# A planned attention and spiking block: counts summed onto x, the first rotation on VectorE, and a plan with varied durations

## The chip, the cores and the metric

The kernel runs on one core of one Trainium2 chip. The metric is device time in microseconds: the median of the runs of one program. The profile is one execution more, taken by the hardware profiler.

## The reference

The input x has 16 batches of 1,024 tokens of 256 features. A causal attention with 16 heads of 16 features and rotary positions, and a spiking feed-forward part, both read the normalised x; both results are added to x.

```python
xn = _layernorm(x, axis=-1)
x = x + _L0_attn_ref(xn, Wq, bq, Wk, bk, Wv, bv, Wo, bo, token_positions) \
      + _L0_ffn_ref(xn, W_fc, W_proj)
# attention: Q, K rotated; softmax(Q K^T / 4, causal) V, then Wo and bo
# feed-forward: 5 steps on the same y
h = jnp.square(jax.nn.relu(jnp.einsum('bsd,fd->bsf', x, W_fc)))
y = jnp.einsum('bsf,df->bsd', h, W_proj)
def step(mem, _):
    reset = spike_fn(mem - THRESHOLD)
    mem_new = BETA * mem + y - reset * THRESHOLD
    return (mem_new, spike_fn(mem_new - THRESHOLD))
_, spks = jax.lax.scan(step, mem0, None, length=NUM_STEPS)
return jnp.sum(spks, axis=0) / NUM_STEPS
```

Since y is the same in all five steps, the number of spikes is a step function of y: the kernel compares y with five constants (`LEAST`) and counts how many it exceeds.

## The kernel before

**Arithmetic.** The f32 factors of a product are split into f16 pairs, a high part and a remainder, and `three` (L587 to L592) makes three f16 matmuls of each product. Weights carry a scale, 256 for the projections and 320 (`WO_S`) for the output projection.

**Stages of a batch.** `norms` reads x two chunks of 128 tokens at a time, normalises, splits into `xhl` and turns it to `xT` by a transposing DMA (L627). `rotated` makes q and k: per half of the tokens and for q and k, two products into PSUM, ACT adds the bias into `qk` (L670), then sine product into `ms` and cosine product into `qk` (L678), difference and sum (L686), the high part on ACT (L733), the remainder (L689), and two stores to a scratch in DRAM, `scr` (L693, L697). `load_slots` brings 4 heads at a time back as `qS` and `kS` (L783). `largest` computes all scores once to find each row's maximum (matmuls L803, VectorE L819 and L837), `weighted` computes them again (L920), takes the exponential on ACT (L981), masks on POOL (L938) and multiplies by the values in f32 (L947); the values carry a column of ones for the softmax sum. Four times per batch a result goes through DRAM to be divided by its sum and split into `ahl`. `forward` is the feed-forward part: product with W_fc, relu and squares on ACT and POOL, product with W_proj into `py`, and `spikes`. `projected` is the output projection: per two chunks one PSUM bank `po`, then `onto` adds it to x, and a DMA stores the result.

**The counts before.** `spikes` writes a f16 tile `count`, by one comparison (L1147) and four that add (L1152), all VectorE over 128x512. Later, in `projected`, TensorE multiplies `count` by a scaled identity `fifth` into `po` ahead of the 12 matmuls of the projection (L1041). There x is loaded (L1066), POOL adds bo (L1068), and VectorE's `onto` adds `po`, over 320, to x (L1059).

**The first rotation before.** `combined` (L381) gives an element-by-element operation to POOL. For batch 0 the rotation is cut in two halves of 512 elements, and each half may be taken by VectorE or by POOL, whichever the plan finds free.

**What sets the order.** Nothing is issued where it is written. `Plan.op` (L155) records an operation with its engine, a planned duration (`cost`), a due time (`when`), and what it reads and writes. `Plan.order` (L193) then plays the whole kernel through with these durations: whenever an engine is free in the plan, it takes the ready operation that is due first, if buffers and PSUM banks allow, and TensorE prefers to stay in its array mode (whole array, split in rows for the scores, split in columns for L947). The order of this play becomes the order of each engine's queue; on the chip every queue runs strictly in that order. Due times come from a period of 140e3 per batch (`BATCH`); the play begins near `S0` = -70e3, and `SMALL` = 60e3 is when wo, bv and bo are loaded. SP issues all DMAs but one, in one queue.

Of the kernel before, what the change touches and what calls it, by code (L numbers as in the profile page):

```python
# [3 lines left out]

# [17 lines left out]
P = 128  # L22
H = 16
# [15 lines left out]
WO_S = 320.0  # L39
# [46 lines left out]
BUFS = dict(w=5, xn=2, x=3, relu=2, ms=2, hT=3, avT=2, ahl=6)  # L86
# [20 lines left out]
SMALL = 60e3  # L107
L1, L2 = 30e3, 25e3
QD = 6.5e3

# [30 lines left out]
class Op:  # L141
    __slots__ = ("mode", "engine", "cost", "when", "what", "held", "waits", "then", "start", "early", "ready", "size", "alt", "name", "patience")


class Plan:
# [9 lines left out]
    def op(self, engine, cost, when, what, reads=(), writes=(), also=(), window=None, size=0.0,  # L155
           alt=(), mode=FULL, patience=PATIENCE):
        o = Op()
        o.mode = mode
        o.size, o.alt, o.patience = size, alt, patience
# [33 lines left out]
    def order(self):  # L193
# [19 lines left out]
        mode = None  # L213

# [50 lines left out]
        while events:  # L265
            now = events[0][0]
            while events and events[0][0] <= now:
                _, _, kind, o = heappop(events)
                if kind == 0:
                    heappush(queues[o.engine], (o.when, o))  # L270
                    if o.alt:
                        heappush(events, (now + o.patience, n, 3, o))
                        n += 1
# [28 lines left out]
            for engine in queues:  # L302
# [7 lines left out]
                if o is not None:  # L310
                    busy[engine] = True
                    o.start = now
                    order.append(o)
                    cost = o.cost
                    if engine == "pe":
                        cost += SWITCH * (o.mode != mode)
                        mode = o.mode
                    heappush(events, (now + cost, n, 1, o))
                    n += 1
# [39 lines left out]
def tile_block(ctx: ExitStack, tc, x, wqkv, bqk, bv, wo, bo, wfc, wproj, cos, sin, out):  # L359
# [21 lines left out]
    def combined(n, when, what, reads, writes, rate=2.27, scalar=None, vector=False):  # L381


        alt, patience = [], PATIENCE
        if scalar is not None:
            alt = [("act", act(n) + 35, scalar)]
        if vector:
            alt, patience = [("dve", dve(n, 2.1), lambda: what(nc.vector))], 0.0
        op("pool", pool_(n, rate), when, lambda: what(nc.gpsimd), reads, writes, alt=alt,
           patience=patience)  # L390
# [46 lines left out]

    fifth = const.tile([P, P], F16, name="fifth")
    nc.vector.tensor_scalar(fifth, ident16, WO_S / NUM_STEPS, None, ALU.mult)

# [106 lines left out]
    def bias_product():  # L547
# [7 lines left out]
    op("dve", dve(D), SMALL + 1e3, lambda: nc.vector.tensor_tensor(bo_sb, pbo.t[:, :D], bo_sb, ALU.add),  # L555
       [pbo, "small"], ["bo"])
# [4 lines left out]
    for i in range(2):  # L561
        t = const.tile([P, NC, H * VW + VT - VW], F32, name=f"v_sb{i}")
        ones = t[:, :, : H * VW].rearrange("p c (h w) -> p c h w", w=VW)[:, :, :, DK]
        nc.gpsimd.memset(ones, 1.0)
        nc.gpsimd.memset(t[:, :, H * VW :], 1.0)
# [9 lines left out]
    class Batch:  # L575
        def __init__(self, b):
# [7 lines left out]
            self.count = [None] * (NC // 2)  # L584
# [10 lines left out]
    def norms(st, times):  # L595
# [36 lines left out]
        for n in range(NC // 2):  # L632
            i = n // (NC // 4)
            t = times[n]
            if n % (NC // 4) == 0:
                for c in range(HALF):
# [14 lines left out]
                   [xn, (hl, 0)], [(hl, 1)], 2.05, vector=b == 0)  # L651
# [3 lines left out]
    def rotated(st, times):  # L655
# [19 lines left out]

        def times_(engine, table, half, to, r, es):
            cols = slice(half * QB, (half + 1) * QB)
            engine.tensor_tensor(  # L678
                to.t[:, es], r.t[:, es],
                table[:, :, cols].broadcast_to([P, es.stop - es.start, QB]), ALU.mult,  # L680
            )

        def added(engine, r, ms, es):
            for e in range(es.start, es.stop):
                a, b = (r.t[:, e, :], ms.t[:, 1 - e, :])[:: 1 if e == 0 else -1]
                engine.tensor_tensor(r.t[:, e, :], a, b, (ALU.subtract, ALU.add)[e])  # L686

        def less(engine, t, r, hl, es):
            engine.tensor_tensor(hl.t[:, 1 - t, es], r.t[:, es], hl.t[:, t, es], ALU.subtract)  # L689
# [12 lines left out]
        for half in range(2):  # L702
            for t in range(2):
# [13 lines left out]
                parts = [slice(0, 1), slice(1, 2)] if b == 0 else [slice(0, 2)]  # L717
                n = 1024 // len(parts)

                def each(after, what, reads, to, mine, rate=2.27):  # L720
                    for es in parts:
                        own = [(to, e) for e in range(2)[es]]
                        combined(n, at + QD + after, lambda e, es=es: what(e, es),
                                 reads if mine is None else [*reads, *((r, e) for e in range(2)[es])],
                                 own, rate, vector=b == 0)

                each(3e3, lambda e, es, half=half, r=r, ms=ms: times_(e, sin_sb, half, ms, r, es),
                     ["sin"], ms, r)
                each(5e3, lambda e, es, half=half, r=r: times_(e, cos_sb, half, r, r, es),
                     ["cos"], r, None)  # L730
                each(8e3, lambda e, es, r=r, ms=ms: added(e, r, ms, es), [(ms, 0), (ms, 1)], r, None)
                op("act", act(1024), at + QD + 10e3,
                   lambda t=t, r=r, hl=hl: nc.scalar.copy(hl.t[:, t], r.t), both, [(hl, t, 0), (hl, t, 1)])  # L733
                for es in parts:
                    es_ = range(2)[es]
                    combined(n, at + QD + 12e3,
                             lambda e, t=t, r=r, hl=hl, es=es: less(e, t, r, hl, es),
                             [*((r, e) for e in es_), *((hl, t, e) for e in es_)],
                             [(hl, 1 - t, e) for e in es_], 2.0, vector=b == 0)
                stored_keys = [(hl, x, e) for x in range(2) for e in range(2)]  # L740
                op("sp", dma(2), at + QD + 13e3, lambda t=t, half=half, hl=hl: stored(t, half, hl),
                   stored_keys, [("scr", b % 2, t, half)], size=move(P * 6 * QB * 2))
# [570 lines left out]
```

## Time and profile before

| | |
|---|---|
| median of 3 runs | 2438.48 us (2437.65 to 2441.66) |
| profiled execution | 2438.26 us, span 2436.6 us |
| mean granted TensorE clock | 0.993 |
| HBM | 122.82 MB read, 101.71 MB written |

The costliest groups (line, engine, operation, written tile, tiles read, shapes, count; then busy time and mean ns of one; then the idle time of the engine just before, with what ended it):

```profile
L981 ACT ACTIVATE w<-banks 128x512 f32<-128x512 f32 (+1 forms) x2560 | 1246.6, 572 | 294.6 <-PE banks L920 280.5
L819 DVE TENSOR_REDUCE nm_sb<-banks 128x1 f32<-128x512 f32 x1024 | 642.6, 683 | 138.8 <-PE banks L803 137.6
L947 PE MATMUL banks<-w,v_sb 128*32 128x512 f32 (+3 forms) x6144 | 622.9, 494 | 3.6 <-DVE nm_sb L819 1.4
```

The granted clock of TensorE over 40 slices of the span, in tenths, and under it the mean busy share of the DMA engines:

```profile
PEclk8999999999999999999999999999999999999999
DMA  5442524433334344344342434233433242432221
```

PE is TensorE's matmuls, PEld its loads of weights, DVE is VectorE, ACT ScalarE, POOL GpSimd and SP the engine that issues DMAs. Matmuls overlap: the duration of one is longer than the time that it holds the array, so the distance from start to start tells its cost. What an idle engine waited for is inferred from semaphores.

### The profile page before, as it was taken

The numbers are of one execution on the slowest core, as the hardware profiler recorded it, in microseconds if no ns is written. First come the engines' busy times: TensorE is split into PE (matmuls) and PEld (weight loads), VectorE is DVE, ScalarE is ACT, GpSimd is POOL, SyncE is SP. The second block draws the span as 40 slices with busy tenths as digits, with TensorE's granted clock in tenths as the row PEclk, the third lists the DMA queues.
The fourth block names the chain that finished last, engine by engine and source line by source line (L and its number), as shares of the span: only waits on it lengthen the run. The fifth ranks groups of instructions, "written<-read, shape, count | busy, mean of one in ns | idle before, by whom it ended". The sixth has DMA issues, their size and how long they took to land.

```text
span 2436.6 us, 59006 instructions
## 1 busy us (share of the span) xinstructions
PE 2356.5 (97%) x21060; PEld 1182.3 (49%) x21060; DVE 1987.8 (82%) x6065; ACT 1843.3 (76%) x3599; POOL 1806.9 (74%) x1922
## 2 busy tenths in 40 slices
PE   5999999999999999999999999999999999999997
PEld 3544444445445445454544445455454444544553
DVE  6888888887987879788788878877878887787882
ACT  5588778787778778777787777787877878777775
POOL 7877757778678877779778587776877858687553
PEclk8999999999999999999999999999999999999999
DMA  5442524433334344344342434233433242432221
GB/s 170 110 102 80 137 80 120 106 89 108 91 119 111 89 100 109 93 110 123 89 115 84 106 113 105 89 96 84 130 98 115 89 103 88 106 113 82 68 68 54
DMA packets 253935, 246.21 MB, mean 101 GB/s; under 512 B 108104, under 2 KB 207816, under 8 KB 253640
## 3 DMA queue, kind: packets, MB, share of 16 engines
q1 hardware_dynamic: 253504, 242.44, 36.2%
q8 instruction: 165, 2.70, 0.5%
q14 instruction: 130, 1.06, 0.2%
q10 hardware_dynamic: 136, 0.00, 0.0%
HBM read 122.82 MB, written 101.71 MB: 92 GB/s over the span
## 4 chain that ended last, share of the span: by engine, by line
PE 58%; DVE 7%; ACT 3%; issue 2%; DMA 1%; POOL 1%; SPq 0%; POOLq 0%; DVEq 0%; ACTq 0%
PE banks L590 27%; PE banks L947 14%; PE banks L920 8%; PE banks L803 8%; DVE junk L837 3%; ACT w L981 2%; DVE nm_sb L819 1%; DVE count L1152 1%; DVE nm_sb L837 1%; PE banks L1041 1%; PE banks L864 0%; ACT hT L1128 0%; POOL hT L1134 0%; DMA av_dram<-avT 0%; DMA inv<-inv 0%
## 5 line engine op out<-in xcount | busy, mean ns | idle before, releaser
L981 ACT ACTIVATE w<-banks 128x512 f32<-128x512 f32 (+1 forms) x2560 | 1246.6, 572 | 294.6 <-PE banks L920 280.5
L819 DVE TENSOR_REDUCE nm_sb<-banks 128x1 f32<-128x512 f32 x1024 | 642.6, 683 | 138.8 <-PE banks L803 137.6
L947 PE MATMUL banks<-w,v_sb 128*32 128x512 f32 (+3 forms) x6144 | 622.9, 494 | 3.6 <-DVE nm_sb L819 1.4
L938 POOL TENSOR_SCALAR_AFFINE_SELECT w<-w 128x256 f32<-128x256 f32 x1024 | 399.3, 408 | 286.9 <-ACT w L981 271.7
L837 DVE CUSTOM_DVE_ANT_0 junk<-banks,mask,nm_sb 128x256 bf16<-128x256 f32 (+3 forms) x1024 | 498.1, 547 | 99.0 <-PE banks L803 61.9
L837 DVE CUSTOM_DVE_ANT_0 junk<-banks,mask 128x256 bf16<-128x256 f32 (+3 forms) x1024 | 444.4, 486 | 64.0 <-PE banks L803 57.2
L920 PE MATMUL banks<-qS,kS 50*128 50x512 f16 (+3 forms) x3072 | 431.7, 328 | 9.6 <-DVE nm_sb L819 3.5
L803 PE MATMUL banks<-kS,qS 48*128 48x512 f16 (+3 forms) x3072 | 415.8, 326 | 9.5 <-DVE nm_sb L837 4.3
L590 PE MATMUL banks<-wproj_hi,hT 128*128 128x256 f16 x2048 | 383.4, 276 | 8.0 <-ACT relu L1123 6.5
L590 PE MATMUL banks<-xT,wfc_hi 128*128 128x256 f16 x2048 | 350.3, 273 | 6.6 <-ACT w L981 2.5
L590 PEld LDWEIGHTS <-hT 128*128 128x128 f16 x3072 | 282.8, 98 | 110.2 <-issue 74.5
L1130 POOL TENSOR_TENSOR relu<-relu 128x1024 f32<-128x1024 f32 x118 | 223.5, 1894 | 125.6 <-ACT hT L1128 125.1
L920 PEld LDWEIGHTS <-kS 50*128 50x128 f16 x3072 | 132.7, 94 | 314.3 <-issue 288.6
L590 PE MATMUL banks<-wproj_lo,hT 128*128 128x256 f16 x1024 | 281.2, 275 | 0.0
L590 PE MATMUL banks<-xT,wfc_lo 128*128 128x256 f16 x1024 | 279.0, 273 | 0.0
L1134 POOL TENSOR_TENSOR hT<-relu,hT 128x1024 f16<-128x1024 f32 x128 | 273.4, 2136 | 2.9 <-ACT relu L1132 0.9
L947 PEld LDWEIGHTS banks<-w,v_sb 128*32 128x32 f32 x6144 | 152.8, 108 | 245.7 <-issue 189.5
L803 PEld LDWEIGHTS <-qS 48*128 48x128 f16 x3072 | 135.7, 94 | 269.7 <-issue 233.5
L1123 ACT ACTIVATE relu<-banks 128x512 f32<-128x512 f32 x256 | 156.1, 610 | 113.9 <-PE banks L590 110.2
L590 PEld LDWEIGHTS <-wfc_hi 128*128 128x128 f16 x2048 | 185.2, 98 | 92.0 <-issue 70.5
L678 POOL TENSOR_TENSOR ms<-qk,sin_sb 128x1024 f32<-128x1024 f32 (+1 forms) x65 | 150.1, 2309 | 70.5 <-ACT qk L670 70.2
L1152 DVE SCALAR_TENSOR_TENSOR count<-banks,count 128x512 f16<-128x512 f32 x256 | 175.2, 684 | 3.6
(84 smaller groups left out, 2820.7 us busy)
## 6 DMA issues: line engine op xcount, KB each, us to landing
av_dram<-avT SPq DMA_DIRECT2D x128, 256.0 KB, 2.1
qS<-scr_q SPq DMA_DIRECT2D x128, 192.0 KB, 3.5
kS<-scr_k SPq DMA_DIRECT2D x128, 192.0 KB, 4.4
x<-in_x_dram SPq DMA_DIRECT2D x66, 256.0 KB, 3.2
scr_q<-qkhl SPq DMA_DIRECT2D x32, 512.0 KB, 3.1
scr_k<-qkhl SPq DMA_DIRECT2D x32, 512.0 KB, 3.0
av<-av_dram SPq DMA_DIRECT2D x64, 256.0 KB, 3.4
inv<-inv SPq DMA_DIRECT2D x64, 256.0 KB, 3.3
```

The lines of the kernel that those rows point to most:

```text
L590: nc.tensor.matmul(out, lhsT=lhs[i], rhs=rhs[j], start=first and n == 0, stop=last and n == 2)
L803: nc.tensor.matmul(pts[two].t[:, at : at + w], lhsT=qS.t[r, h, c * P : (c + 1) * P], rhs=kS[r, h, k0 : k0 + w], start=True, stop=True,)
L819: lambda two=two, pt=pt: nc.vector.tensor_reduce(nm0[:, two, i, c : c + 1], pt.t, axis=AX.X, op=ALU.max),
L837: nc.vector.tensor_tensor_reduce(next(junk)[:, :w], pt.t[:, at : at + w], mask[:, QB - w :], scale=1.0, scalar=nm0[:, two, i, chunk] if pa ...
L920: nc.tensor.matmul(pts[two].t[:, at : at + n], lhsT=kS[r, i, j * P : (j + 1) * P], rhs=qS.t[r, i, qb * QB + off : (qb + 1) * QB], start=Tr ...
L938: nc.gpsimd.affine_select(out=d, in_=d, compare_op=ALU.is_ge, fill=0.0, base=0, pattern=[[0, 2], [1, P]], channel_multiplier=-1,)
L947: nc.tensor.matmul(pav.t[VT * h : VT * (h + 1), off:], lhsT=st.v[:, j, col : col + VT], rhs=ws[h % 2].t[:, h // 2, at : at + QB - off], st ...
L981: lambda n=n, two=two, pt=pt, w=w: nc.scalar.activation(w.t[:, two, :n], pt.t[:, :n], AF.Exp, scale=SCALE),
L1123: lambda r=r, ph=ph, pr=pr: nc.scalar.activation(r.t[:, 2 * pr : 2 * pr + 2].rearrange("p f t -> p (f t)"), ph.t, AF.Relu, scale=1.0 / WS),
L1130: combined(1024, when + 4e3, lambda e, r=r: e.tensor_tensor(r.t, r.t, r.t, ALU.mult), [], [(r, 0), (r, 1)], 1.75, lambda r=r: nc.scalar.ac ...
L1134: lambda e, r=r, hT=hT: e.tensor_tensor(hT.t[:, 1], r.t, hT.t[:, 0], ALU.subtract),
L1152: lambda step=step: nc.vector.scalar_tensor_tensor(flat(count), py.t, least[step], flat(count), ALU.is_gt, ALU.add),
```

## The change

1. `spikes` no longer has a tile of its own: all five comparisons add to the tile of x (f32). For this, `forward` now loads x, ACT multiplies it by 5, and POOL adds 5 times (bo and the bias of the values); `projected` loads nothing and has no matmul with `fifth`; `onto` takes x over 5 plus `po`. The ones in the values become 4, which leaves `ahl` a quarter of what it was, and `WO_S` becomes 4, so that `po` needs no scale. There are 9 buffers of x in place of 3, and no `count`.
2. The rotation of batch 0 (and its remainder of xn) is recorded for VectorE, whole, and not for POOL with VectorE as an alternative.
3. `Plan.order` multiplies each planned duration by a random factor between 0.97 and 1.03; for each half batch of planned time the generator starts from a seed of the list `DRAWN`. It changes the planned order alone.
4. wo, bv and bo are due at -20e3 in place of 60e3; the memsets of `kS` may start after the second tile of normalised x and not the fourth.

```diff
-WO_S = 320.0
+WO_S = 4.0
-BUFS = dict(w=5, xn=2, x=3, relu=2, ms=2, hT=3, avT=2, ahl=6)
+BUFS = dict(w=5, xn=2, x=9, relu=2, hT=3, avT=2, ahl=6)
-SMALL = 60e3
+SMALL = -20e3
+VARIED, STRETCH = 0.03, BATCH / 2
+DRAWN = [
+    0, 0, 1, 5, 3, 4, 6, 6, 4, 4, 7, 0, 0, 6, 0, 1, 7, 0, 4, 5, 6, 5, 5, 3, 7, 6, 0, 7, 2, 5, 1, 0, 2, 0,
+]
...
+        drawn, change, varied = list(DRAWN), -1e9, None
...
         while events:
             now = events[0][0]
+            if now >= change:
+                varied = Random(drawn.pop(0) if drawn else 0)
+                change = S0 + STRETCH if change < S0 else change + STRETCH
...
+                    cost *= varied.uniform(1 - VARIED, 1 + VARIED)
                     heappush(events, (now + cost, n, 1, o))
...
-        if vector:
-            alt, patience = [("dve", dve(n, 2.1), lambda: what(nc.vector))], 0.0
+        if vector:
+            op("dve", vector * 70 + n * 1.06, when, lambda: what(nc.vector), reads, writes)
+            return
...
+        nc.vector.tensor_tensor(bo_sb, pbo.t[:, :D], bo_sb, ALU.add)
+        nc.vector.tensor_scalar(bo_sb, bo_sb, float(NUM_STEPS), None, ALU.mult)
...
-        nc.gpsimd.memset(ones, 1.0)
+        nc.gpsimd.memset(ones, WO_S)
...
-                parts = [slice(0, 1), slice(1, 2)] if b == 0 else [slice(0, 2)]
+                one, two = ((1, 2) if b == 0 else (0, 0))
+                combined(1024, at + QD + 3e3,
+                       lambda e, half=half, r=r, ms=ms: times_(e, sin_sb, half, ms, r),
+                       [*both, "sin"], [ms], vector=one)
+                combined(1024, at + QD + 5e3,
+                       lambda e, half=half, r=r: times_(e, cos_sb, half, r, r), ["cos"], both,
+                       vector=one)
+                combined(1024, at + QD + 8e3, lambda e, r=r, ms=ms: added(e, r, ms), [ms], both,
+                         vector=two)
...
         def product(c, po):
-            nc.tensor.matmul(
-                po.t, lhsT=fifth, rhs=st.count[c // 2].t.rearrange("p c d -> p (c d)"),
-                start=True, stop=False,
-            )
...
         def onto(n, po):
-            nc.vector.scalar_tensor_tensor(xc, po.t, 1.0 / WO_S, xc, ALU.mult, ALU.add)
+            nc.vector.scalar_tensor_tensor(xc, xc, 1.0 / NUM_STEPS, po.t, ALU.mult, ALU.add)
...
         def spikes(t, py, when):
+            x_ = st.x[t]
+            for step in range(NUM_STEPS):
+                def counted(step=step):
+                    xc = x_.t.rearrange("p c d -> p (c d)")
+                    nc.vector.scalar_tensor_tensor(
+                        xc, py.t, WS * LEAST[step], xc, ALU.is_gt, ALU.add)
+                op("dve", dve(512), when + 2e3 + 200 * step, counted, [py], [x_])
...
-                        st.count[t - 1] = held("count", 8, shape, F16, f"count_{b}_{t - 1}")
+                        st.x[t - 1] = x_ = load_x(b, t - 1, "x", times[0] - 15e3)
+                        op("act", act(2 * D), times[0] - 8e3,
+                           lambda x_=x_: nc.scalar.mul(x_.t, x_.t, float(NUM_STEPS)), [], [x_])
+                        op("pool", pool_(2 * D), times[0] - 6e3,
+                           lambda x_=x_: nc.gpsimd.tensor_tensor(
+                               x_.t, x_.t,
+                               bo_sb.rearrange("p (o d) -> p o d", o=1).broadcast_to([P, 2, D]),
+                               ALU.add), ["bo"], [x_])
...
-                   [st.ready[3]], [("kS", i)])
+                   [st.ready[1]], [("kS", i)])
```

## The prediction

> **What bounds the kernel now.** I read the busy shares first, then the chain of waits, then the busy time of each engine in stretches of the span, and last the order in time around the places that the change touches.
>
> ```profile
> span 2436.6 us, 59006 instructions
> PE 2356.5 (97%) x21060; PEld 1182.3 (49%) x21060; DVE 1987.8 (82%) x6065; ACT 1843.3 (76%) x3599; POOL 1806.9 (74%) x1922
> PE 58%; DVE 7%; ACT 3%; issue 2%; DMA 1%; POOL 1%; SPq 0%; POOLq 0%; DVEq 0%; ACTq 0%
> ```
>
> TensorE is busy for all but 80 us, and the chain that ended last is mostly TensorE. The stretches (their columns: PE, PEld, DVE, ACT, POOL busy, granted clock, DMA share, GB/s) tell where the 80 us lie:
>
> ```profile
> 0.00:20.00 20.00, 3.54 (x17) 2.27 (x18) 11.17 (x35) 10.90 (x24) 6.81 (x20) 1.00 0.69 214
> 20.00:40.00 20.00, 15.82 (x93) 9.17 (x92) 17.80 (x22) 14.14 (x19) 18.50 (x12) 0.90 0.52 152
> 40.00:60.00 20.00, 11.73 (x77) 8.47 (x76) 10.77 (x9) 10.07 (x16) 19.69 (x14) 0.76 0.41 137
> 60.00:80.00 20.00, 19.38 (x144) 13.66 (x143) 13.19 (x49) 9.11 (x15) 15.28 (x10) 0.91 1.05 211
> ...
> 300.00:600.00 300.00, 296.06 (x2683) 146.70 (x2676) 253.55 (x808) 235.94 (x466) 222.17 (x243) 1.00 0.34 98
> ```
>
> The first 60 us hold 28.9 us of TensorE's idle time (16.46 + 4.18 + 8.27), and there POOL is the full engine, with the first rotation. From 120 to 2380 us the idle time is 32.9 us in all, some 4 us in 300. So in the body the time is TensorE's work, and in the opening it is the way from the first x to the first scores.
>
> **The matmul of the counts goes.** 64 matmuls of 128x512 (L1041) leave TensorE's queue. Their 388 ns each is latency, so I take the step from start to start:
>
> ```profile
> 1116.02 0.39 PE L1041 MATMUL banks<-count,fifth 128*128 128x512 f16 x1
> 1116.25 0.27 PE L590 MATMUL banks<-wo_hi,ahl 128*128 128x256 f16 x1
> ...
> 1117.45 0.27 PE L590 MATMUL banks<-wo_hi,ahl 128*128 128x256 f16 x1
> 1117.65 0.28 PE L920 MATMUL banks<-qS,kS 50*128 50x256 f16 x2
> ```
>
> 1116.25 - 1116.02 is 0.23; another, inside a group, took 0.22 (2416.70 to 2416.92). 64 x 0.22 = -14.1 us, on the engine that sets the end. The same lines price the next term: a 256-column matmul steps by 0.11 within its group, and 0.20 where the row-split scores follow it, so a change of array mode costs about 0.09.
>
> **The drawn plan.** The draw changes no instruction, only the order that the planner writes into each queue. In the built programs TensorE changes between full, row-split and column-split matmuls 2,355 times before and 2,366 times after: 11 x 0.09 = +1.0 us. What the order does to waits the trace can't show; idle in the four stretches of 300 us from 300 to 1500 us is 3.9, 4.5, 2.5 and 3.5, then 6.7 and 4.7, a spread of 1.4. Over 7.5 such stretches that is 1.4 x sqrt(7.5), some 4 us either way, which I take as the bound for a new order; value 0.
>
> **The first rotation on VectorE.** Before, it is halved, and POOL and VectorE each take parts. POOL's last part ends at 56.4, SP issues the last store of k at 56.44, and the first score starts 12.9 later:
>
> ```profile
> 33.47 0.68 DVE L686 TENSOR_TENSOR qk<-qk,ms 128x512 f32<-128x512 f32 x1
> 34.08 1.21 DVE L491 SCALAR_TENSOR_TENSOR wproj_lo<-wproj_stage,wproj_hi 128x1024 f16<-128x1024 f32 x1
> ...
> 45.44 1.75 DVE L678 TENSOR_TENSOR qk<-qk,cos_sb 128x512 f32<-128x512 f32 x1
> ```
>
> ```profile
> 69.33 0.28 PE L803 MATMUL banks<-kS,qS 48*128 48x256 f16 x1
> ```
>
> The new order gives VectorE four sets of sin, cos, subtract, add and remainder: 3 x 1.21 + 2 x 0.68 = 5.0 each (1.21 is the row for two-input work of 1,024 elements), 20.0 together. Between them stand two remainders of wproj (2.4), five statistics of the next batch (5 x 0.59) and one pair of rstd and mr (2 x 0.3): 26.0. It can start when both halves of the first qk are in (24.0 before) and the second wfc remainder is through (24.35 before), say 25. With no collision it ends at 51, 5.4 before POOL's 56.4. But the same 512-element operation takes 0.68 or 1.75; the long ones stand where POOL reads SBUF too, 1.07 more. If all 20 collide it ends at 72.4, +16.0. In the new order POOL has in this stretch an x addition (1.27), two rstd and mr pairs (1.3), two remainders of xn (1.15), two squares (1.89), two remainders of hT (2.1) and one sine (2.31), 16.5 us, so about half of the time; half of 20 at 0.8 is 8. I take 59, +2.6, between -5.4 and +16.0.
>
> The Trainium skill, "SBUF — State Buffer", section "SBUF: two separate sides", speaks against this step: VectorE with two SBUF inputs and GpSimd lock one port pair for a whole instruction, and the loser waits. The trace agrees, as far as 0.68 against 1.75 can show it; the worst that this lock could do is priced in rival B.
>
> **What is put ahead of the first transposes.** SP now issues four x loads, the five small loads and one more xn before or between them. The issues (4 x 0.47 and 5 x 0.6) end near 10 us, before the transposes' data is there (13.04 before). The bytes are 1.4 MB, 4.6 us at the 300 GB/s of 4 to 8 us; between 8 and 14 us the DMA engines have 3.3 us to spare (shares 0.53, 0.50, 0.30). So +1.3, bounds 0 and +4.6. The bias matmuls now stand first on TensorE (four passes, 1.0 us), inside its 16.46 us of waiting; nothing is queued behind but work that waits for the same transposes.
>
> Against that, the new order puts 89,600 columns before the first score, the old 76,800. 12,800 x 0.11/256 = 5.5 us of filling work done earlier. Opening: +2.6 + 1.3 - 5.5 = -1.6, from -10.9 to +15.1.
>
> **x behind the counts.** The five count operations write f32 x where they wrote f16 count: both read one bank; the rows are 684 ns for count, 688 for x (L1059), so 0. The addition of bo stays POOL's. New are 64 multiplications by 5 on ACT, 128x512 at 0.60 each (the copy of xn): 38 us, covered by ACT's 593 us of idle time; uncovered they would be 38 us. They bring a wait: load, ACT, POOL, counts now stand in a row in three in-order queues, and behind an ACT instruction that waits for x stand the exponentials (L981), behind these TensorE. Before, POOL's addition did that waiting:
>
> ```profile
> L1068 POOL TENSOR_TENSOR x<-x,bo_sb 128x512 f32<-128x512 f32 x64 | 81.3, 1274 | 25.4 <-DMA x<-in_x_dram 12.6 <-DVE nm_sb L819 9.8 <-DVE nm_sb L837 3.0
> ```
>
> 12.6 us in 6 waits. If ACT inherits it, TensorE loses between 0 and 12.6; exponentials mostly wait for TensorE (280.5 us), not the other way, so I take +1. The nine x buffers wait for a store two batches back, as the three did; 0. The kS memsets only move earlier on POOL, and the second multiplication of bo is one operation; 0.
>
> **Sum.** The profiled execution took 2438.26 us with a span of 2436.6; the median of the runs is 2438.48, so the one stands for the other within 0.01%. 2438.26 - 14.1 + 1.0 - 1.6 + 1 = 2424.6; I say 2424.
>
> **Rivals.**
> A, slower: the ACT queue waits for x. From 15 us of loss, 0.23 us for each of 64 chunks, it outweighs the gain. For it: the load now needs to land before ACT, POOL and VectorE in turn, and landings of x run from 2.1 to 5.7 us. Against: the loads stand early in SP's order. If a third of the 64 wait 2.1 us (12.6/6), 44 us, and half of that reaches TensorE: 2424.6 - 1 + 22 = 2446.
> B, hardly any change: the opening collides at every operation. +15.1 in place of -1.6: 2424.6 + 16.7 = 2441. For it: every second VectorE operation of the old rotation is a long one. Against: POOL has half as much to do there. If each of the 20 lost a whole POOL operation (1.72, POOL's L678 where both engines work), the rotation would end at 85.4, the opening cost 29.0 + 1.3 - 5.5 = +24.8, and the time would be 2451.
> C, hardly any change: the matmuls were hidden, since in the body VectorE would bind in TensorE's place. For it: VectorE at 98% from 70 to 120 us. Against: 82% over the span, and TensorE's waits on it from 120 to 2380 us sum to some 17 us. All 14.1 comes back: 2438.
> D, much faster: the draw removes half of the body's 32.9 us, and the rotation doesn't collide (-5.4 in place of +2.6): 2424.6 - 16.4 - 8.0 = 2400. For it: three of six stretches come near 4 us, one has 2.5. Against: the waits are scattered over many releasers, none above 6 us.
> That the counts stay off x is none: 320 operations on x stand in the built program.
>
> **How the numbers follow.** Forecast 0.53, A 0.17, B 0.10 (0.03 of it the 2451), C 0.08, D 0.12. The likeliest's own range is 2414 to 2436: the order's 4, and most of the opening's bounds. The range of 8 in 10 goes down to 2404, near D, and up to 2447, over A's price. A measurement tells 0.2%, 4.9 us, from no change, so faster is below 2433.6 and slower above 2443.4. Faster: 0.53 + 0.12 + some 0.05 of the milder ends of B and C = 0.70. Same: most of B and C, 0.10. Slower: A and the rest of B, 0.20.
>
> **What would show it.** Right: no L1041; 64 new multiplications on ACT with few microseconds of waiting for x; TensorE's busy time near 2342; the first score between 64 and 75 us; VectorE's 1,024-element operations between 1.2 and 2.3; idle of TensorE near 4 us in 300 in the body. Wrong: exponentials that wait behind an ACT multiplication, TensorE's idle time in the body above 50 us, VectorE above 90% there, or a first score after 85 us.

## The result and the profile after

The changed kernel takes 2431.09 us (median of 6 runs, 2426.26 to 2433.15) against 2438.43 us for the kernel before on the same chip: a ratio of 0.9965, with a 95% interval of 0.9956 to 0.9975, or 8.5 us less; the two medians alone lie 7.3 us apart. It is faster, by 0.35%. The profiled execution took 2432.1 us. The profiled executions of the kernels below lie up to 5 us from their own medians, one of them 7, so that differences of some 3 us between single profiles say little.

First the head of the page of the changed kernel: its span, the busy time of each engine, and the chain of waits.

```profile
span 2430.4 us, 58976 instructions
PE 2344.1 (96%) x20996; PEld 1175.5 (48%) x20996; DVE 2000.4 (82%) x6070; ACT 1878.6 (77%) x3671; POOL 1769.9 (73%) x1897
PE 15%; DVE 2%; ACT 1%; issue 1%; DMA 0%; POOL 0%; POOLq 0%; SPq 0%; DVEq 0%; ACTq 0%
```

TensorE has 64 instructions fewer and is busy 12.4 us less, but the span fell by 6.2 us only. Half of what TensorE no longer does has become time in which it waits. (The chain's shares sum to under 20% here, so the shares of this view can't be set beside those of before.) The stretches of the changed kernel, in the columns shown before (PE, PEld, DVE, ACT, POOL busy, granted clock, DMA share, GB/s), tell where it waits:

```profile
0.00:20.00 20.00, 0.00 (x0) 0.00 (x0) 9.73 (x34) 7.56 (x17) 8.96 (x22) 1.00 0.79 190
20.00:40.00 20.00, 16.23 (x82) 9.53 (x83) 13.85 (x24) 15.23 (x24) 10.70 (x7) 1.00 0.82 223
40.00:60.00 20.00, 13.15 (x78) 8.47 (x78) 19.79 (x20) 12.84 (x20) 9.95 (x5) 0.83 0.55 132
...
300.00:600.00 300.00, 297.99 (x2702) 143.36 (x2700) 255.42 (x792) 245.21 (x484) 227.73 (x245) 1.00 0.37 103
```

TensorE does nothing in the first 20 us, where it had 3.54 us of work before. From 40 to 60 us VectorE is the full engine, at 19.79 of 20, where POOL was. In the body the stretch from 300 to 600 us has 2.0 us of idle time, where it had 3.9.

For the rest of the text I divide TensorE's idle time into three parts: 0 to 120 us (the opening), 120 to 2380 us (the body), and what follows. Each is the width of the stretch less its PE entry; the last is the rest of the span.

| one profiled execution | span | PE busy | idle, opening | idle, body | idle, end |
|---|---|---|---|---|---|
| before | 2436.6 | 2356.5 | 31.3 | 32.9 | 15.9 |
| changed | 2430.4 | 2344.1 | 36.9 | 34.8 | 14.6 |

So -12.4 of work, +5.6 of waiting in the opening, +1.9 in the body and -1.3 at the end. The 12.4 is itself good to some 2.5 us: with TensorE's work and order unchanged, another profile (the run without ACT's multiplications, below) has 2341.6 us of busy time where this one has 2344.1.

**The opening.** This is SP's order in time in the changed kernel (start, duration of the group, line, tile, count):

```profile
5.51 2.45 SPq L429 DMA_DIRECT2D x<-in_x_dram  x3
8.79 0.60 SPq L534 DMA_DIRECT2D wo_stage<-in_wo_dram  x1
...
15.89 0.54 SPq L535 DMA_DIRECT2D bv_sb<-in_bv_dram  x1
19.55 0.35 SPq L537 DMA_DIRECT2D bo_sb<-in_bo_dram  x1
20.48 0.37 SPq L429 DMA_DIRECT2D x<-in_x_dram  x1
21.53 1.37 SPq L636 DMA_TRANSPOSE xT<-xhl  x1
```

The issues do not end near 10 us. From the eleventh on they are held, by up to 3 us each, and the first transpose goes out at 21.53 us, where it went out at 13.04. SP's own waits in the first 30 us of the same kernel name what held them (in all, times, longest):

```profile
SPq L537 <- DMA sin_sb<-in_sin_dram: 3.1, 1, 3.1
...
SPq L535 <- DMA cos_sb<-in_cos_dram: 1.4, 1, 1.4
...
SPq L535 <- DMA x<-in_x_dram: 0.9, 1, 0.9
SPq L534 <- DMA wqkv_stage<-in_wqkv_dram: 0.8, 1, 0.8
```

The load of bo has no data in common with that of the sine table, yet it waits for it. Counted in SP's order, wo is the 12th issue and waits for the 4th (wqkv), the second bv is the 15th and waits for the 7th (cos), bo is the 16th and waits for the 8th (sin): each issue waits until the eighth before it has landed. The wait stands in the program: in the trace the issue of bo waits for the semaphore that the landing of the sine table counts up, and uses the same one for its own landing. The program has eight such semaphores for these DMAs and hands them out in turn, so the runs show no limit of the chip here. The kernel before had just eight issues ahead of its first transpose. Behind that stands TensorE, which begins with the bias product, and the first scores:

```profile
23.75 2.07 PE L555 MATMUL banks<-wo_stage,bv_wide 128*128 128x256 f32 x4 [23.75 <-DVE bv_wide L550]
25.62 0.42 PE L599 MATMUL banks<-wqkv_hi,xT 128*128 128x256 f16 x1
```

```profile
25.55 1.50 PEld L599 LDWEIGHTS <-xT 128*128 128x128 f16 x8 [0.44 <-DMA xT<-xhl]
```

```profile
79.94 0.27 PE L797 MATMUL banks<-kS,qS 48*128 48x256 f16 x1 [1.45 <-DMA kS<-scr_k]
```

The first matmul is 7.3 us later than before (16.46), the first that reads xT 9.2 us, and the first score 10.6 us (69.33). The weight load from xT waits for the transposed tile until 25.55, as the bias product ends, so the bias product itself holds back next to nothing here.

**The first rotation.** VectorE's order in time, some of the rows of L686 (sine and cosine), L691 (difference) and L732 (remainder); TENSOR_TENSOR reads two tiles:

```profile
34.48 1.21 DVE L686 TENSOR_TENSOR ms<-qk,sin_sb 128x1024 f32<-128x1024 f32 x1
...
56.03 2.36 DVE L686 TENSOR_TENSOR qk<-qk,cos_sb 128x1024 f32<-128x1024 f32 x1
58.32 3.14 DVE L732 TENSOR_TENSOR qkhl<-qk,qkhl 128x1024 f16<-128x1024 f32 x1
61.38 2.38 DVE L691 TENSOR_TENSOR qk<-qk,ms 128x512 f32<-128x512 f32 x1
...
65.47 1.23 DVE L732 TENSOR_TENSOR qkhl<-qk,qkhl 128x1024 f16<-128x1024 f32 x1 [0.21 <-ACT qkhl L730]
```

It runs from 34.48 to 66.70, 32.2 us. Most 1,024-element operations take 1.2 us. The long ones stand in two places, 43 to 49 us and 56 to 64 us, and POOL's order in time has its wide operations just there:

```profile
42.58 3.76 POOL L658 TENSOR_TENSOR xhl<-xn,xhl 128x512 f16<-128x512 f32 x2 [2.69 <-ACT xhl L655]
46.31 1.71 POOL L1146 TENSOR_TENSOR x<-x,bo_sb 128x512 f32<-128x512 f32 x1
55.40 1.91 POOL L1113 TENSOR_TENSOR relu<-relu 128x1024 f32<-128x1024 f32 x1 [7.38 <-ACT hT L1111]
57.39 2.99 POOL L1117 TENSOR_TENSOR hT<-relu,hT 128x1024 f16<-128x1024 f32 x1
60.34 2.87 POOL L1113 TENSOR_TENSOR relu<-relu 128x1024 f32<-128x1024 f32 x1
```

The ends show more than the durations. POOL's three operations from 55.40 on end at 57.31, 60.38 and 63.21, and VectorE's three long ones at 58.39, 61.46 and 63.76: 1.08, 1.08 and 0.55 us later, close to what the same operations take alone (1.2 and 0.7). The three long ones of the first place end 1.08, 0.55 and 0.55 us after an operation of POOL's. So each looks as if it did its work only when POOL's was over. From 48.02 to 55.40 POOL does nothing, and VectorE's operations of the rotation there take 1.2 and 0.7 us. POOL's two operations on 128x4, from 37.51 to 39.89, did not lengthen VectorE's beside them (0.68 and 1.22).

**The counts on x.** From the groups of the changed kernel:

```profile
L1128 DVE SCALAR_TENSOR_TENSOR x<-banks,x 128x512 f32<-128x512 f32 x320 | 219.0, 684 | 46.0 <-PE banks L599 39.1 <-POOL qkhl L732 1.5 <-POOL w L932 1.4
L1146 POOL TENSOR_TENSOR x<-x,bo_sb 128x512 f32<-128x512 f32 x64 | 83.6, 1310 | 23.1 <-ACT x L1144 17.9 <-DVE bo_sb L564 5.1
L1144 ACT ACTIVATE x<-x 128x512 f32<-128x512 f32 x64 | 42.3, 663 | 7.0 <-DMA x<-in_x_dram 7.0
```

The 320 count operations take 684 ns each, what they took on the f16 tile. The 64 multiplications cost ACT 42.3 us and wait 7.0 us for x, in two waits that both lie in the opening. POOL, which waited 12.6 us for x before, now waits 17.9 us for ACT.

### The profile page after: what moved, and what is told of

It is laid out like the page before. It is cut to its first block, busy times and chain, and to the rows that moved or that the text cites. A ratio compares the mean times of both kernels' runs of the same rounds, so it can differ in the third digit from the quotient of the medians.

```text
span 2430.4 us, 58976 instructions
## 1 busy us (share of the span) xinstructions
PE 2344.1 (96%) x20996; PEld 1175.5 (48%) x20996; DVE 2000.4 (82%) x6070; ACT 1878.6 (77%) x3671; POOL 1769.9 (73%) x1897
## 5 line engine op out<-in xcount | busy, mean ns | idle before, releaser
L1113 POOL TENSOR_TENSOR relu<-relu 128x1024 f32<-128x1024 f32 x111 | 211.1, 1902 | 160.6 <-ACT hT L1111 160.3
L1128 DVE SCALAR_TENSOR_TENSOR x<-banks,x 128x512 f32<-128x512 f32 x320 | 219.0, 684 | 46.0 <-PE banks L599 39.1
L686 POOL TENSOR_TENSOR ms<-qk,sin_sb 128x1024 f32<-128x1024 f32 x60 | 142.0, 2367 | 47.6 <-ACT qk L679 47.6
```

Source lines behind the costliest of these rows:

```text
L1113: combined(1024, when + 4e3, lambda e, r=r: e.tensor_tensor(r.t, r.t, r.t, ALU.mult), [], [(r, 0), (r, 1)], 1.75, lambda r=r: nc.scalar.ac ...
L1128: nc.vector.scalar_tensor_tensor(xc, py.t, WS * LEAST[step], xc, ALU.is_gt, ALU.add)
```

## The experiments

The first theory, from the two traces: the matmuls' 12 us came off; the loads put ahead of the transposes cost the opening its 5.6 us; the body lost a little to the new order. Most parts were then tried alone. All ratios are to the kernel before, on the same chip in the same batch. The changed kernel was not run again in these batches, so a comparison with it is one of two ratios.

**Loads behind the transposes.** The planned order is kept, but the four x loads of batch 0 and the loads of wo, bv and bo are placed behind the last load of wproj, and what depends on them behind the last store of the first rotation.

```diff
+    def placed_later(order, loads, rest):
+        early = [o for o in order if o.tag in loads]
+        late = [o for o in order if o.tag in rest]
+        order = [o for o in order if o.tag not in (*loads, *rest)]
+        a = next(n for n, o in enumerate(order) if o.tag == "wproj 1") + 1
+        order[a:a] = early
+        c = next(n for n, o in enumerate(order) if o.tag == "stored 0 1 1") + 1
...
+        order[c:c] = late
+        return order
-    for o in plan.order():
+    for o in placed_later(plan.order(), ('small load', 'x load'), ('small', 'x mul', 'x add')):
```

> The order of the changed kernel, with one cut: the four x loads of batch 0 and the five small loads (wo, bv, bo) stand on SP behind the loads of wproj, and what reads them (the four multiplications, the four additions, the bias product and its neighbours) behind the last store of the first rotation. Theory Q (in the changed kernel the first transposes are issued at 21.5 us in place of 13.0 because SP's issues of these loads wait, each for a DMA eight issues older to land): the first transpose goes out near 14, the first matmul of TensorE starts at 17 to 18 in place of 23.75, the first score at 70 to 73 in place of 79.9, and the time is 7 to 10 us below the changed kernel, 2421 to 2424. Rival R (the start of the chain sets nothing, since VectorE's rotation takes its 32 us wherever it begins and TensorE has filling work): the first score moves but the time stays within 3 us of 2431.

Then the same with one half of the loads each: `('small load',), ('small', 'x add')` and `('x load',), ('x mul', 'x add')`.

> As the kernel with both groups moved, but only the five small loads (0.4 MB) and what reads them stand late; the four x loads (1.0 MB) and their multiplications stay ahead of the first transposes. If the count of issues ahead is what holds SP (theory Q: a transpose waits for the DMA eight issues before it), the first transpose is now the thirteenth issue and waits for a load issued fifth, landed by 12.2: first transpose at 14 to 15.5, and most of the gain, time 2422 to 2426. If the bytes are what holds it (Q'), a good two thirds of the delay stays: first transpose at 18 to 20, time 2427 to 2430.

> The other half: the four x loads of batch 0, their multiplications and additions stand late; the five small loads and the bias product stay ahead. By count (Q) the first transpose is the fourteenth issue and waits for the sixth, near 14: first transpose at 14.5 to 16, time 2422 to 2426, unless the small loads are slow to land and hold the bias product that stands first on TensorE. By bytes (Q') 0.4 of 1.4 MB stay ahead: first transpose at 15 to 17, time 2423 to 2426. What tells Q from Q' is this run against the one with the small loads late: equal by Q, this one better by Q'.

| | median us | ratio, 95% interval | first transpose issued | first matmul | idle, opening |
|---|---|---|---|---|---|
| changed | 2431.09 | 0.9965 [0.9956, 0.9975] | 21.53 | 23.75 | 36.9 |
| all loads late | 2426.54 | 0.9949 [0.9934, 0.9963] | 14.37 | 17.76 | 33.2 |
| wo, bv, bo late | 2430.15 | 0.9963 [0.9949, 0.9976] | 14.62 | 22.78 | 36.1 |
| x late | 2431.68 | 0.9966 [0.9953, 0.9979] | 14.39 | 21.68 | 36.2 |

With all of them late, SP and TensorE begin nearly as they did before the change; TensorE's first row:

```profile
17.76 0.40 PE L600 MATMUL banks<-wqkv_hi,xT 128*128 128x256 f16 x1 [17.76 <-DMA xT<-xhl]
```

The first score comes at 72.77 us, 7.2 us earlier than in the changed kernel, but the time falls by some 4 us only (0.9965 to 0.9949; the two intervals overlap), less than the 7 to 10 that were expected. The halves were to tell whether the number of outstanding DMAs or their bytes held the opening. For the issue of the transpose it is the number: each half alone lets it go out at 14.4 to 14.6 us. But neither time falls to the expected 2422 to 2426, since TensorE begins only at 21.68 to 22.78 us. Two other things take over, and two profiles show them. With x still early, the transposed data is the late one:

```profile
22.78 0.39 PE L600 MATMUL banks<-wqkv_hi,xT 128*128 128x256 f16 x1 [22.78 <-DMA xT<-xhl]
```

The transposed tile is there 8.2 us after the issue began, where it took 3.4 us with all loads late. With wo, bv and bo early, TensorE's first instruction is the bias product, and the products of xT stand behind it in the queue until bv has come:

```profile
21.68 2.08 PE L556 MATMUL banks<-wo_stage,bv_wide 128*128 128x256 f32 x4 [21.68 <-DVE bv_wide L551]
```

So three things can hold the opening: the issues, the loads of x still under way ahead of the transposed data, and the place of the bias product in TensorE's queue. Taking away one leaves the next. That it is the bytes of the x loads, and not their number, was not tried.

**The matmuls alone.** The kernel before, in its own order, without the 64 matmuls of the counts:

```diff
-            nc.tensor.matmul(
-                po.t, lhsT=fifth, rhs=st.count[c // 2].t.rearrange("p c d -> p (c d)"),
-                start=True, stop=False,
-            )
...
-                        False, j == 1 and k == KD - 1,
+                        k == 0, k == KD - 1,
```

> The kernel before, in its own order, without the 64 matmuls of the counts (the output lacks the spikes). Theory W (TensorE's work sets the body, each matmul costs its step of 0.22): 14 us less, 2423 to 2426, TensorE's busy time near 2343 and its idle time near 80 as before. Rival C (the matmuls were covered, VectorE binds in their place): 2434 to 2438, and TensorE's idle time grows by what its busy time loses.

It takes 2435.97 us: 0.9985, 0.9976 to 0.9994, which is 3.8 us less and not 14. Its span is 2433.9 us, and its busy times are:

```profile
PE 2344.0 (96%) x20996; PEld 1176.7 (48%) x20996; DVE 1987.0 (82%) x6065; ACT 1843.7 (76%) x3599; POOL 1805.8 (74%) x1922
```

TensorE's busy time falls by 12.5 us, as it should. The idle time grows by 10: 2.2 in the opening (the first matmul was 1.5 us later in this execution), 1.2 at the end, and 6.4 in the body, from 32.9 to 39.3. TensorE's waits from 120 to 2380 us show who ends them; the kernel before, then the one without the matmuls (what waited and for what; us in all, times, longest):

```profile
PE banks L590 <- ACT w L981: 5.8, 11, 1.0
PE banks L803 <- DVE nm_sb L837: 3.8, 8, 1.3
PE banks L920 <- DVE nm_sb L819: 3.5, 4, 2.8
...
PE banks L1041 <- ACT w L981: 1.4, 4, 0.5
```

```profile
PE banks L590 <- ACT w L981: 7.5, 16, 1.1
PE banks L803 <- DVE nm_sb L837: 4.0, 8, 1.3
PE banks L920 <- DVE nm_sb L819: 3.9, 6, 2.1
...
PE banks L803 <- DVE nm_sb L819: 2.0, 2, 1.8
```

No single wait takes the place of the matmuls. Nearly every row grows a little: the split products (L590), the output projection's among them, now meet the wait for the exponentials that L1041 met (5.8 + 1.4 before, 7.5 now), and the scores wait longer for VectorE's maxima. Summed over all rows of this view by what ended the wait, VectorE goes from 17.2 to 21.5 us, ScalarE from 8.8 to 9.6 and DMAs from 0.4 to 1.5: two thirds of the new waiting is behind VectorE, spread over many small waits.

**The matmuls put back.** The changed kernel, with 64 matmuls of a zero tile into the same banks:

```diff
+    zeros = const.tile([P, P], F16, name="zeros")
+    nc.gpsimd.memset(zeros, 0.0)
...
+            nc.tensor.matmul(
+                po.t, lhsT=zeros, rhs=wo_hi.rearrange("p k d -> p (k d)"), start=True, stop=False,
+            )
...
-                        k == 0, k == KD - 1,
+                        False, j == 1 and k == KD - 1,
```

> The changed kernel in its own order, with 64 matmuls of 128x512 of zeros put where the count matmuls stood (one ahead of each output projection; the output is the same). If a matmul costs TensorE's whole step wherever the order is good (W): 14 us more, 2443 to 2447. If most of it is filled into TensorE's waits, as taking it out of the kernel before gave 3.8 us: 2434 to 2437. Between them, near 2440: the chosen order leaves less room than the old one.

It takes 2435.43 us: 0.9988, 0.9978 to 0.9998, against the changed kernel's 0.9965 some 5.6 us more. TensorE's busy time rises by 7.5 us here, to 2351.6, and not by 12.5, which is more than single profiles of one order differ by and isn't explained. Both ways the matmuls are worth 4 to 6 us, under half of the 12.5 us of busy time that went with them at the fixed order of before.

**Less work for VectorE.** If the amount of VectorE's work bound the body next to TensorE, taking some from it should help. The kernel before, without the last of the five comparisons:

```diff
                 op("dve", dve(512), at,
+                   (lambda: None) if step == NUM_STEPS - 1 else
                    lambda step=step: nc.vector.scalar_tensor_tensor(
```

> The kernel before, in its own order, without the fifth of the five comparisons per tile: 64 operations of 684 ns, 43.8 us of VectorE's work, are left out (the output lacks the fifth spike), and TensorE's work is untouched. If TensorE alone sets the body (the prediction's view): 2437 to 2440, no change. If VectorE's queue sets a good part of it (what the run without the count matmuls suggests, where 14 us of TensorE's work gave 3.8): 10 us or more less, below 2430.

VectorE's busy time falls from 1987.8 to 1955.2 us, and the time is 2438.73 us: 1.0004, 0.9994 to 1.0014. In the order of before, with its matmuls, 33 us of VectorE's work is worth nothing.

**The draw.** The changed kernel with `VARIED = 0.0`:

> The changed kernel with the planned durations not varied (0 in place of 0.03); its opening has the same order of loads. The run without the matmuls gave back only 3.8 us of 14, and moving the loads 4 to 5, so of the change's 8.5 us a remainder of some 9 has no source but the order. Theory D (the drawn order is what makes the kernel faster): 2437 to 2443, within 0.2% of the kernel before, with more idle time of TensorE in the body than the changed kernel's 34.8 us. Rival T (a plan made without the matmul, and counts that go onto x, are worth it under any order): 2429 to 2434.

and with two other lists of seeds, `Random(10 + ...)` and `Random(20 + ...)` in place of `Random(...)`:

> The changed kernel with other seeds (10 added to each). Theory D (the chosen list is a lucky one): 2435 to 2445, slower than the changed kernel by 4 us or more. Rival T: within 3 us of the changed kernel, 2428 to 2434. Theory N of the prediction (an order is worth 4 us either way, centre at no effect): between 2427 and 2435.

> Other seeds again (20 added to each). Theory D: 2435 to 2445. Rival T: 2428 to 2434. Together with the two runs before it, it shows how far apart orders of the same work lie; by the prediction's bound of 4 us the three should lie within 8 us of each other.

| order of the changed kernel | median us | ratio, 95% interval | mode changes | PE busy | idle, opening | idle, body |
|---|---|---|---|---|---|---|
| the list | 2431.09 | 0.9965 [0.9956, 0.9975] | 2366 | 2344.1 | 36.9 | 34.8 |
| not varied | 2437.14 | 0.9996 [0.9987, 1.0004] | 2346 | 2342.3 | 35.8 | 43.8 |
| seeds + 10 | 2431.19 | 0.9970 [0.9956, 0.9984] | 2364 | 2341.7 | 35.2 | 36.5 |
| seeds + 20 | 2436.96 | 1.0000 [0.9988, 1.0013] | 2375 | 2343.8 | 37.2 | 38.5 |

This is the main finding. Without the draw, everything else that the change does is worth 1 us, within the interval. That agrees with the parts: some 4 to 6 us won by the matmuls, some 4 lost by the early loads. The draw of the list is worth 7.6 us (0.9996 to 0.9965). One of two other lists is as good, the other worth nothing. The list has 20 array-mode changes more than the unvaried order; 1.8 us more of busy time would be 0.09 for each, but seeds + 10 have 18 more and 0.6 us less, so these profiles can't show that price. The gain is the body's idle time, 43.8 to 34.8. (The profile of the unvaried order is an execution 3.3 us above its median, so part of the 9.0 may belong to that execution.) The body of the unvaried order, over 120 to 2380 us, and then that of the list (columns of the stretches):

```profile
120.00:2380.00 2260.00, 2216.21 (x20081) 1103.76 (x20081) 1891.79 (x5825) 1777.18 (x3497) 1678.98 (x1807) 1.00 0.36 100
```

```profile
120.00:2380.00 2260.00, 2225.24 (x20159) 1104.61 (x20157) 1903.54 (x5848) 1789.60 (x3519) 1673.53 (x1812) 1.00 0.36 100
```

In the same 2,260 us TensorE gets through 78 instructions more. The waits of the unvaried order are again many small ones; the largest are the split products, one line for all projections, behind the maxima and the exponentials:

```profile
PE banks L599 <- DVE nm_sb L831: 7.2, 19, 1.2
PE banks L599 <- ACT w L975: 5.1, 13, 1.0
```

The list's order has 3.6 and 1.0 us there, and in exchange a longer wait of the second scores for the maxima (7.6 us against 4.6). Summed over all rows, the waits behind ScalarE are 7.5 us in the unvaried order and 1.8 in the list's, those behind VectorE 28.0 and 23.0.

**The list on the kernel before.** The same draw, with the same seeds, in the planner of before:

```diff
+            if now >= change:
+                varied = Random(drawn.pop(0) if drawn else 0)
+                change = S0 + STRETCH if change < S0 else change + STRETCH
...
+                    cost *= varied.uniform(1 - VARIED, 1 + VARIED)
```

> The kernel before with the varied plan and the same list of seeds added, nothing else. In it TensorE changes its array mode 2,395 times, 40 more than in the kernel before, some 4 us. If the list is good for any plan: 2428 to 2434. If an order is a draw whose worth holds for one program only (theory D): anywhere between 2432 and 2446, not near -8 us; I expect 2440.

2446.88 us: 1.0032, 1.0021 to 1.0044, 8 us slower, and above the 2432 to 2446 that were expected. It has 2,395 mode changes (40 more), a PE busy time of 2362.1 us (5.6 more) and 41.4 us idle in the body (8.5 more) in a profiled execution of 2453.9 us, 7 us above its median. The list that goes with a gain in one program goes with a loss in this one.

**ACT's multiplications.** The changed kernel's order, with the 64 multiplications left out:

```diff
+        if o.tag == "x mul":
+            continue
```

> The changed kernel in its own order, without ACT's 64 multiplications of x by 5 (x enters the output at a fifth). 42.3 us of ACT's work go, and with them ACT's 7.0 us of waiting for x, all of it in the opening. The prediction's term (ACT's idle time covers them; +1): within 2 us of the changed kernel, 2429 to 2433. Rival A of the prediction (waits for x and 0.66 us ahead of exponentials reach TensorE): 8 us or more less, below 2424.

2428.53 us: 0.9957, 0.9941 to 0.9973, against 0.9965 some 2 us less, inside the intervals. They cost little or nothing.

**Late loads and other seeds together.** The loads of the first experiment, with seeds + 10:

> The version with the late loads of batch 0, and 10 added to each seed. The late loads gave 4.3 us under the chosen list, the other seeds 1 us less than it. If the two add up: 2426 to 2429. If the late loads were worth what they were only for that order: 2429 to 2434.

2425.28 us: 0.9944, 0.9929 to 0.9959. Against the same seeds with early loads (0.9970, 0.9956 to 0.9984) that is 6 us less, with intervals that just overlap, and the opening's idle time falls from 35.2 to 31.5 us, by the same 3.7 us as in the first experiment (36.9 to 33.2). It is the lowest median of this study, 13.5 us below the kernel before; it stands level with the late loads under the list (0.9949). Its profiled execution has 31.5 us of idle time in the opening and 34.3 in the body.

## Why the prediction was right, and where it was not

The forecast was 2424 us, in a range of 2404 to 2447, with 0.70 on faster. It came out at 2431.09 and faster. The range held, and so did the sign, but in good part by luck. The three largest errors of the sum partly cancel, and the term that brought the gain, the draw, had been valued at nothing: without it the same change came out at 0.9996. Term by term:

| step of the sum | forecast | measured |
|---|---|---|
| matmuls of the counts | -14.1 | -3.8 taken out, +5.6 when put back |
| the draw | +1.0 of mode changes, order 0 +/- 4 | -7.6 against the unvaried order |
| opening | -1.6 | +5.6 of idle time, 3.7 of it from the early loads |
| ACT's multiplications | +1 | +2, inside the interval |
| counts on x | 0 | 0 by their duration (684 ns) |

*The matmuls.* The step "64 x 0.22 = -14.1 us, on the engine that sets the end" failed in its second half. The price of the work was right: TensorE's busy time fell by 12.4 us, to 2344 where 2342 was forecast. That the time would follow was not. The text read 97% busy and 4 us of idle time in 300 as a body that is TensorE's work alone. With the same queues, a TensorE that comes earlier finds its inputs not ready: 6.4 us of the body's gain went into many small waits, two thirds of them behind VectorE. The likely reason, which no run isolates, is that the plan lets each input be ready about when TensorE comes to it, so a short wait does not mean that there was room. That is what rival C said of the outcome, for the matmuls alone: some 10 of the 14 us came back. Of its ground, that VectorE would bind, the waits bear out that TensorE now waits for VectorE's maxima, but not that the amount of VectorE's work sets the time: 33 us less of it, with the matmuls in place, moved nothing. Whether the same relief would help once the matmuls are gone wasn't tried.

*The draw.* Value 0 was taken, with 4 us either way, from the spread of idle time between stretches. Four orders of the same changed kernel lie between ratios of 0.9965 and 1.0000, 8.5 us apart, so the size of the bound was about right. What was wrong is the point it was laid around: the sum took the changed program, unvaried, to keep the body's idle time of before, 32.9 us, but its order has 43.8 in the one profile of it, and the draw brought back most of what that had lost. Why the unvaried order of the new work is so much worse than that of the old isn't shown. Rival D spoke of a draw that takes half of the body's idle time. In that it was half right, since the draw did take 9.0 us, but from 43.8, not from 32.9, and so nothing came of its 2400.

*The opening.* Three terms made -1.6. The rotation's length was well judged: 34 us forecast (25 to 59), 32.2 measured, and its 1,024-element operations lay between 1.19 and 3.14 us where 1.2 to 2.3 was expected; the worst of rival B, a loss at every operation, did not come. Its start failed, at 34.48 and not at 25. The step at fault is "the issues end near 10 us, before the transposes' data is there", with its +1.3 and the bounds 0 and +4.6. It priced issues and bytes and left out the wait of each issue for the eighth before it, and with 17 issues ahead the transposed data itself came 4.0 us after its issue, at 25.5. That "the bias matmuls" would fit "inside its 16.46 us of waiting" left out that bv lands only at 23 us; they also took 1.9 us (23.75 to 25.62), not 1.0. In the changed kernel this cost little, since the data of xT came as late; with x late it held TensorE. The first matmul came 7.3 us later, and the first score at 79.94, outside the 64 to 75 that were named. That only 5.6 us of idle time came of 10.6 us of delay agrees with the work put ahead of the scores, which was priced at 5.5 us.

The page "SBUF — State Buffer" of the Trainium skill, section "SBUF: two separate sides", was weighed against the rotation: a VectorE operation with two SBUF inputs and a GpSimd one lock each other out for the whole instruction. The trace agrees for POOL's wide operations: all six long operations of the rotation stand beside one, each ends 0.55 or 1.08 us after POOL's has ended, and none stands where POOL is idle. Together they lost 7.8 us (2.17, 2.36 and 3.14 against 1.21; 1.64, 1.75 and 2.38 against 0.68), where the forecast took ten losses of 0.8. A loss at each of the twenty would need a POOL that is never idle.

*ACT and x.* Rival A, exponentials behind an ACT multiplication that waits for x, fell. ACT's 7.0 us of waiting lie in the opening, and without the multiplications the time is the same within its interval.

The Trainium skill, "Perfetto Trace Analysis", section "Identifying the Most-Contended Engine", holds that TensorE's headroom is to be judged by its arithmetic and its weight loads, not by the busy time of its matmuls, and that the engine of highest occupancy is to be worked on first. The runs fit the first half as far as they go: 12.4 us of busy time gave 4 to 6; the share of its arithmetic was not worked out here. Read by the weight loads, 49%, TensorE would stand behind VectorE with its 82%; but 33 us less of VectorE's work gave nothing.

What stays open: which waits a given order shortens, since only their sums differ clearly between the orders and each single one is below a few microseconds; and what the rotation on VectorE does alone, which wasn't tried apart from the rest.

## What to carry to other kernels

In a kernel whose queues are planned to the last slot, the busy share of the fullest engine prices the work that is taken from it only as an upper bound: take the work out at a fixed order and look at what the waits do. Before an edit is credited with a fraction of a per cent, run it under several equally good orders, since the order alone moved this kernel by 0.35%. And ahead of the first transfer that matters, look which older DMA its issue has to wait for, here the eighth before it, and do not count only the time of issues and bytes.

## What the hardware showed that was not expected

- A semaphore that the program uses again is enough to hold a DMA queue: the 16th issue on SP stood 3.1 us for the 8th, with which it shares no data, and the first transpose went out at 21.53 us in place of 13.04.
- VectorE's operations with two inputs in SBUF, beside a wide operation of POOL's, ended 0.55 us (512 elements) or 1.08 us (1,024) after POOL's had ended, and took up to 3.14 us in place of 1.21.
- Loads ahead of a transposing DMA delay its data as well as its issue: 8.2 us from issue to use with four more loads of x issued ahead, 3.4 us without.
- 12.4 us less busy time on an engine that is busy 97% gave 4 to 6 us, and 33 us less on one that is busy 82% gave nothing measurable (1.0004, 0.9994 to 1.0014).
